# Layer 0 of a four-layer block: routing cut in two parts around its counts, with conv steps, the other half's norms and shared products placed between the parts

## The chip, the core and the metric

The kernel runs on one core of one Trainium2 chip. The metric is device time in microseconds (us). The kernel before takes 1593.74 us as the median of 3 runs (1591.17 to 1594.62).

A core has five engines that each run their own list of instructions in order: PE (TensorE, matmuls, with PEld for its weight loads), DVE (VectorE), ACT (ScalarE), POOL (GpSimd) and SP (SyncE, which here only issues DMAs). They meet at semaphores. An instruction that waits holds up everything behind it on its own engine.

## The reference, cut to what matters

Four layers, each `x = x + attn(norm(x)) + ffn(norm(x))`, on 4096 tokens (16 sequences of 256) of 128 float32 values. Only layer 0 is touched. Its attention is a diagonal state-space recurrence, its feed-forward a mixture of 8 experts with top-2 routing plus one shared expert:

```python
xn = layernorm(x)                                # over 128
# L0 attn: a linear recurrence over time, y = scan(...) @ W_out + b_out
# L0 ffn:
logits = layernorm(xn) @ gate_w.T                # 8 experts
probs = softmax(logits); tk_probs, tk_idx = top_k(probs, 2)
tk_probs = tk_probs / (sum(tk_probs) + 1e-5)
out = swiglu(xn, sWg, sWu, sWd)                  # the shared expert
for e in range(8):
    out = out + w[:, e:e+1] * swiglu(xn, Wg[e], Wu[e], Wd[e])
```

Since the recurrence is linear and the same for all tokens, it is a convolution of each of the 128 channels with a fixed kernel of 256 lags.

## The kernel before, in words

**Tiling.** The tokens lie in 8 blocks `X[0..7]` of 128 x 4 x 128. Layer 0 treats them in two halves (hf 0: blocks 0 to 3, hf 1: blocks 4 to 7), each of 16 row tiles (`HN`).

**What layer 0 does**, by name of its helpers:

- `plain(hf, n, True)` writes a block's normalised rows `xn` by ACT, 4 instructions (L249); `bare(hf, n)` writes the rows that feed the convolution into `Z`, also 4 ACT instructions of L249.
- `turned(hf, n)` transposes a block of `xn` on PE (L149) and copies it to `xT` by ACT (L263). `router(hf, n)` multiplies it with the gate on PE (tile `lg`) and scales it into `logits` on DVE (L280).
- `route(hf)` turns a half's logits into expert slots. Its first part (L311 to L329) is softmax and two arg-maxima, 20 DVE instructions with one exponential on ACT (L314) between them, and ends in `per`, each partition's count per expert. Then PE sums the counts (`tot`, `pos`). The second part (L338 to L382) is DVE again: running positions, tile starts, `slots` (L368), the experts of the slot tiles (`rows_of`, L377), and the two weights of each token (L378 to L382).
- `scatter(hf, n, k)` (L389) sends rows of `xn` to their slots in DRAM (`XS`): 32 indirect DMAs a half, issued by POOL. They need `slots`.
- `toeplitz(g)` (L495) loads a 512 KB tile of lags by SP; 8 buffers, shared with the experts' weights. `conv(q)` does a 16-channel step of the convolution: 64 matmuls into one bank (`cv`), a copy on ACT (L513), a store by SP (L517). It needs all of `Z` and four of the lag tiles. `mix_in(q)` issues the loads for two steps further on and then runs `conv(q)`.
- `share(q)` adds `xn` to block q (L666, DVE) and runs the shared expert: `pg`, `pu` on PE (512 columns, 4 pairs), Silu on ACT (L528), the product on DVE (L529), `py` on PE, and the sum on DVE (L535).
- `lag_levels()` works out what beta and the output bias add: `kf` on ACT (L470), `wb` and `mix` on DVE (L472, L473), PE `lagd`, ACT copy (L478), PE `level`, DVE (L483).

After that come 46 expert tiles of 256 slots each (23 a half): SP loads weights `we` and rows `xs` six tiles ahead, PE does `xsT`, `sg`, `su`, `sy`. Layers 1 to 3 follow.

**What sets the order.** Inside `tc.manual_schedule(engines=ordered)` PE, ACT, DVE and SP keep the order in which the calls are written; POOL is free. Where two such blocks meet, a planner may interleave the end of one with the start of the next on an engine.

**PSUM.** All of layer 0 takes banks from one ring of 8 in the order of allocation, so a new tile waits until the reader of the eighth before it is done.

The written order around the change is: `bare` of all blocks, `route(0)`, scatters of half 0; then a second block: `mix_in(0)`, `plain`/`turned`/`router` of half 1, `mix_in(1)`, `share(0)`, `mix_in(2)`, `share(1)`, `route(1)`, `lag_levels`; scatters of half 1; then a third block with `share(2)` to `share(7)` and `mix_in(3)` to `mix_in(7)` in turn.

Of the kernel before, what the change touches and what calls it, by code (L numbers as in the profile page):

```python
# [51 lines left out]
def program(ctx: ExitStack, tc: tile.TileContext, x, consts, consts0, rows, pk0, w0s, w0e, pk1, pk1i, pk2, pk3, out):  # L52
# [7 lines left out]
    def bank(name):  # L60
        return psum["now"].tile([P, 512], F32, tag="ps", name=name)
# [48 lines left out]
    def mm(o, l, r, start=True, stop=True):  # L110
        nc.tensor.matmul(o, l, r, start=start, stop=stop)  # L111
# [26 lines left out]
    def normalise(dst, src, mv, r, at):  # L138
        for t in range(NT):
            nc.vector.tensor_scalar(  # L140
                dst[:, t, :], src[:, t, :], mv[:, at + t, 0:1], r[:, at + t : at + t + 1],
                ALU.subtract, ALU.mult,
            )
# [45 lines left out]
    with early, banks(8, 0), tc.tile_pool(name="l0", bufs=2) as sp:  # L189
# [15 lines left out]
        for hf in range(2):  # L205
# [3 lines left out]
            n = TILES * SLOTS // P  # L209
# [12 lines left out]
        def clear(hf):  # L222
            for o, i in fills[hf]:
                zeroed[hf].append(nc.sync.dma_start(out=o, in_=i))
# [23 lines left out]
        def rows_by_act(dst, src, r, off, k):  # L248
            nc.scalar.activation(dst, src, AF.Identity, bias=off[:, k : k + 1], scale=r[:, k : k + 1])  # L249

        def plain(hf, n, by_act):
            i = HALVES[hf][n]
            mv, r, _, off, _, _ = mvs[hf]
            if by_act:
                for t in range(NT):
                    rows_by_act(xn[i][:, t, :], X[i][:, t, :], r, off, n * NT + t)
            else:
                normalise(xn[i], X[i], mv, r, n * NT)
# [12 lines left out]
        def router(hf, n):  # L271

            i = HALVES[hf][n]
            if hf not in lgs:
                lgs[hf] = small("logits", hf, HN, E)
            lg = bank(f"lg{i}")
            for t in range(NT):
                mm(lg[:, t * E : (t + 1) * E], xT[i][:, t * P : (t + 1) * P], gates[:, 0])
            ks = slice(n * NT, (n + 1) * NT)
            V.tensor_tensor(  # L280
                lgs[hf][:, ks, :], lg[:, 0 : NT * E].rearrange("p (t e) -> p t e", e=E),
                mvs[hf][5][:, ks].unsqueeze(2).to_broadcast([P, NT, E]), ALU.mult,
            )
# [15 lines left out]
        def route(hf):  # L299


            red = lambda name: sp.tile([P, HN], F32, tag=name, name=f"{name}{hf}", bufs=1)
            full = lambda name: sp.tile([P, HN, E], F32, tag=name, name=f"{name}{hf}", bufs=1)
            per_e = lambda name, *shape: sp.tile([P, *shape], F32, tag=name, name=f"{name}{hf}", bufs=1)
# [22 lines left out]
            V.tensor_tensor(both, oh1, oh2, ALU.add)  # L327
            per = per_e("per", E)
            V.tensor_reduce(per, both.rearrange("p n e -> p e n"), AX.X, ALU.add)  # L329
            tot = bank(f"tot{hf}")  # L330
            mm(tot[:, 0:E], ones2, per)
            pos = bank(f"pos{hf}")
# [88 lines left out]
        def lag_powers():  # L421
            for k in ("fine", "coarse"):
                t = parts[k] = sp.tile([P, 64, 16], F32, tag="h", name=f"lag_{k}", bufs=2)
                V.tensor_tensor(
                    t, parts["rate"].unsqueeze(2).to_broadcast([P, 64, 16]),
                    W0[k].unsqueeze(1).to_broadcast([P, 64, 16]), ALU.mult,
                )
                nc.scalar.activation(t, t, AF.Exp)
# [39 lines left out]
        def lag_levels():  # L468

            nc.scalar.copy(kf, bass.AP(tensor=kb.tensor, offset=kb.offset + 2 * P - 1, ap=[list(kb.ap[0]), [-1, 2 * P]]))  # L470
            wb = sp.tile([P, D], F32, tag="wb", name="wb", bufs=1)
            V.tensor_scalar(wb, W0["wout"], W0["beta"], None, ALU.mult)  # L472
            V.tensor_scalar(mix, W0["wout"], W0["gamma"], None, ALU.mult)  # L473
            ps = bank("lagd")
            for h in range(2):
                mm(ps[:, h * D : (h + 1) * D], kf[:, h * P : (h + 1) * P], wb)
            g = sp.tile([P, 2, D], F32, tag="kb", name="lagd", bufs=1)
            nc.scalar.copy(g, ps[:, 0 : 2 * D].rearrange("p (h d) -> p h d", h=2))  # L478
            ps = bank("level0")
            for h in range(2):  # L480
                for k, (w, at) in enumerate(((W0["upper"], h), (ident, h), (ones2, 0))[0 : 2 + h]):
                    mm(ps[:, h * D : (h + 1) * D], w, g[:, at], k == 0, k == 1 + h)
            V.tensor_tensor(  # L483
                level0, ps[:, 0 : 2 * D].rearrange("p (h d) -> p h d", h=2),
                W0["bout"].unsqueeze(1).to_broadcast([P, 2, D]), ALU.add,
            )
# [4 lines left out]
        def toeplitz(g):  # L491

            toes[g] = sp.tile([P, 4, 256], F32, tag="blk", name=f"toe{g}", bufs=8)
            src = bass.AP(tensor=kd.tensor, offset=kd.offset + g * 4 * 384, ap=[[1, P], [384, 4], [1, 256]])
            return nc.sync.dma_start(out=toes[g], in_=src)  # L495

        def conv(q):

            ps = bank(f"cv{q}")
            for n in range(4):
                toe = toes.pop(4 * q + n)
                for at, k in ((1, 128), (0, 0)):
                    for c in range(4):
                        u = Z[:, at : at + 2, :, 16 * q + 4 * n + c].rearrange("p h b -> p (h b)")
                        mm(
                            ps[32 * c : 32 * c + 32, n * P : (n + 1) * P], u, toe[:, c, k : k + P],
                            n == 0 and at == 1, n == 3 and at == 0,
                        )  # L510
            y = sp.tile([P, 4, P], F32, tag="yc", name=f"yc{q}")
            back = bass.AP(tensor=ps.tensor, offset=ps.offset + P - 1, ap=[list(ps.ap[0]), [P, 4], [-1, P]])
            nc.scalar.copy(y, back)  # L513
            dst = bass.AP(
                tensor=ycd.tensor, offset=ycd.offset + 16 * q * B * S, ap=[[P, P], [4 * B * S, 4], [1, P]]
            )
            nc.sync.dma_start(out=dst, in_=y)  # L517
# [101 lines left out]

        AHEAD = 6  # L620
        NJ = len(jobs)
        ordered = {mybir.EngineType.PE, mybir.EngineType.Activation, mybir.EngineType.DVE, mybir.EngineType.SP}
        with tc.manual_schedule(engines=ordered):
            nc.sync.dma_start(out=kd[:, 256:384], in_=zero[:, 0, :])
            clear(0)
            lag_rates(spread)
            lag_powers()
            spread(0, (1,))
            lag_states()
            lag_sums()  # L630
            spread(0, (2, 3))
            scales(0)
            lag_rows()
            gate_parts()
            plain(0, 0, True)
            plain(0, 3, False)
            plain(0, 1, True)
            turned(0, 0)
            plain(0, 2, True)
            turned(0, 3)  # L640
            turned(0, 1)
            bare(0, 0)
            turned(0, 2)
            spread(1, range(4))
            scales(1)
            for n in (0, 3, 1, 2):
                router(0, n)
            for g in range(8):
                toeplitz(g)
            clear(1)  # L650
            for n in range(1, 4):
                bare(0, n)
            for n in range(4):
                bare(1, n)
            route(0)
        for n in range(HN):
            for k in range(2):
                scatter(0, n, k)

        def mix_in(q):  # L660
            for g in range(4 * q + 8, min(4 * q + 12, 32)):
                toeplitz(g)
            conv(q)

        def share(q):
            V.tensor_tensor(X[q], X[q], xn[q], ALU.add)  # L666
            shared_expert(q)
# [3 lines left out]
            V.tensor_tensor(x4, x4, level0.unsqueeze(1).to_broadcast([P, 2, 2, D]), ALU.add)  # L671

        with tc.manual_schedule(engines=ordered):
            mix_in(0)
            for n in range(4):
                plain(1, n, True)
                turned(1, n)
                if n > 0:
                    router(1, n - 1)
            mix_in(1)  # L680
            router(1, 3)
            share(0)
            mix_in(2)
            share(1)
            route(1)
            lag_levels()
        for n in range(HN):
            for k in range(2):
                scatter(1, n, k)
# [16 lines left out]
        with tc.manual_schedule(engines=ordered | {mybir.EngineType.Pool}):  # L706
# [6 lines left out]
            norms = []  # L713
            for k in range(NJ):
                if k + AHEAD < NJ:
                    fetch_weights(k + AHEAD)
                n = k - TILES - 1
                if 0 <= n < 12:
                    fetch_outputs(0, n)
                if k + AHEAD < NJ:  # L720
                    fetch_slots(k + AHEAD)
                if k + 2 < NJ:
                    turn_slots(k + 2)
                if k + 1 < NJ:
                    up_slots(k + 1)
# [767 lines left out]
```

## Time and profile before

| | |
|---|---|
| median of 3 runs | 1593.74 us |
| the profiled execution | 1487.93 us, of which its span 1486.2 us |
| mean granted TensorE clock of the profiled execution | 0.940 |
| PE busy in the span | 1340.1 us (90%) |
| DVE, ACT, POOL busy | 752.8, 578.4, 214.3 us |
| PE busy, 36.5 to 43.0 us | 0.00 of 6.50 us |
| PE busy, 43.0 to 50.2 us | 1.58 of 7.20 us |
| PE busy, 79.7 to 95.5 us | 7.97 of 15.80 us |
| PE busy, 95.5 to 109.3 us | 5.27 of 13.80 us |
| PE busy, 113 to 157 us | 40.86 of 44.00 us |
| PE busy, 185 to 260 us | 75.00 of 75.00 us |

The profile is of one execution, and all times of single instructions come from it. It ran 106 us faster than the median of the timed runs. Its rows give start, duration, engine, source line, tile and count; "idle before <-X" is how long that engine stood still and which event ended it. Times are counted from the start of the span. In the chain of work that ended last PE holds 79%, DVE 10% and ACT 7%.

### The profile page before, as it was taken

The numbers are of one execution on the slowest core, as the hardware profiler recorded it, in microseconds if no ns is written. First come the engines' busy times: TensorE is split into PE (matmuls) and PEld (weight loads), VectorE is DVE, ScalarE is ACT, GpSimd is POOL, SyncE is SP. The second block draws the span as 40 slices with busy tenths as digits, with TensorE's granted clock in tenths as the row PEclk, the third lists the DMA queues.
The fourth block names the chain that finished last, engine by engine and source line by source line (L and its number), as shares of the span: only waits on it lengthen the run. The fifth ranks groups of instructions, "written<-read, shape, count | busy, mean of one in ns | idle before, by whom it ended". The sixth has DMA issues, their size and how long they took to land.

```text
span 1486.2 us, 28149 instructions
## 1 busy us (share of the span) xinstructions
PE 1340.1 (90%) x11950; PEld 868.6 (58%) x11950; DVE 752.8 (51%) x1636; ACT 578.4 (39%) x898; POOL 214.3 (14%) x218
## 2 busy tenths in 40 slices
PE   3659999969898999899999999999979999999995
PEld 3546899836565666656555445554546666666434
DVE  7355444756666555335732336423375565554364
ACT  5412223334353554321343334333344545543551
POOL 1366004323110000000220112211100000000013
PEclk9979999977798999899999999999978999997998
DMA  7849669640000000000000000000000000000001
GB/s 225 283 135 312 205 178 278 197 152 21 10 11 2 2 2 2 2 1 1 0 1 0 1 0 1 0 0 0 0 1 2 2 2 2 2 2 2 1 1 57
DMA packets 71007, 77.92 MB, mean 52 GB/s; under 512 B 7649, under 2 KB 60258, under 8 KB 70242
## 3 DMA queue, kind: packets, MB, share of 16 engines
q1 hardware_dynamic: 66210, 66.39, 14.5%
q0 software_dynamic: 4240, 8.99, 1.8%
q8 instruction: 94, 1.54, 0.4%
q10 hardware_dynamic: 432, 0.75, 0.2%
q14 instruction: 31, 0.25, 0.1%
HBM read 55.46 MB, written 20.64 MB: 51 GB/s over the span
## 4 chain that ended last, share of the span: by engine, by line
PE 79%; DVE 10%; ACT 7%; issue 2%; DMA 1%; POOL 1%; POOLq 0%; DVEq 0%; SPq 0%; ACTq 0%
PE h L111 15%; PE se L111 9%; PE sc L111 8%; PE po L111 7%; PE av L111 5%; ACT E L920 4%; DVE M L878 3%; PE c L111 3%; PE mT L893 3%; PE sy L111 3%; PE sg L111 2%; PE su L111 2%; PE pq L111 2%; PE pv L111 2%; PE b L111 2%; PE a L111 2%
## 5 line engine op out<-in xcount | busy, mean ns | idle before, releaser
L878 DVE TENSOR_REDUCE M<-sc 128x4 f32<-128x1024 f32 (+3 forms) x256 | 195.9, 818 | 105.0 <-PE sc L111 105.0
L111 PE MATMUL h<-h,pk 128*128 128x512 f32 x512 | 221.0, 592 | 0.0
L920 ACT ACTIVATE E<-se 128x1024 f32<-128x1024 f32 (+1 forms) x192 | 158.8, 879 | 126.0 <-PE se L111 125.7
L111 PEld LDWEIGHTS h<-h,pk 128*128 128x128 f32 x512 | 97.3, 190 | 119.0 <-issue 114.8
L111 PE MATMUL sc<-Kp,Qm 32*128 32x192 f32 (+3 forms) x2048 | 139.8, 358 | 25.0 <-ACT E L920 19.9
L111 PE MATMUL se<-Q,Km 32*128 32x256 f32 (+3 forms) x2048 | 138.4, 355 | 22.4 <-DVE M L878 20.9
L111 PEld LDWEIGHTS sc<-Kp,Qm 32*128 32x128 f32 x2048 | 103.5, 207 | 74.6 <-ACT E L920 33.4
L111 PEld LDWEIGHTS se<-Q,Km 32*128 32x128 f32 x2048 | 99.3, 202 | 62.9 <-issue 51.8
L1098 ACT ACTIVATE h<-h,pk 128x512 f32<-128x512 f32 x64 | 44.0, 687 | 144.3 <-PE h L111 144.2
L1048 POOL TENSOR_TENSOR pr<-q,k 128x512 f32<-128x512 f32 (+2 forms) x24 | 28.3, 1205 | 495.7 <-ACT k L1041 285.8
L601 POOL DMA_INDIRECT yk<-YS,slots x64 | 60.7, 949 | 225.9 <-DMA YS<-ys 95.0
L1108 DVE TENSOR_TENSOR x<-x,po 128x512 f32<-128x512 f32 x8 | 5.5, 688 | 170.5 <-PE po L111 170.5
L111 PE MATMUL av<-E,vals 128*32 128x256 f32 (+3 forms) x2048 | 77.7, 304 | 0.0
L389 POOL DMA_INDIRECT XS<-xn,slots x64 | 63.0, 985 | 73.4 <-DVE slots L368 48.3
L1240 POOL TENSOR_TENSOR xT<-xT,c 128x512 f32<-128x512 f32 x8 | 10.2, 1271 | 389.8 <-DVE c L1239 380.4
L935 ACT COPY cu<-av 128x512 f32<-128x512 f32 x32 | 18.8, 586 | 120.6 <-PE av L111 120.6
L111 PEld LDWEIGHTS av<-E,vals 128*32 128x32 f32 x2048 | 52.9, 111 | 20.0 <-issue 1.6
L583 DVE TENSOR_TENSOR hs<-hs,su 128x512 f32<-128x512 f32 x46 | 31.6, 686 | 57.3 <-PE su L111 57.3
L899 DVE TENSOR_TENSOR Q<-Qp,mT 128x512 f32<-128x512 f32 x32 | 22.0, 688 | 58.0 <-PE mT L893 58.0
L111 PE MATMUL pk<-xT,pk 128*128 128x512 f32 x80 | 47.0, 672 | 3.8 <-ACT Qm L812 3.7
L819 DVE TENSOR_SCALAR Km<-Kp,consts 128x512 f32<-128x512 f32 x64 | 32.2, 545 | 34.6 <-ACT Kp L817 34.6
L111 PEld LDWEIGHTS sy<-we,hs 128*128 128x128 f32 x368 | 47.6, 192 | 2.4 <-DVE hs L583 0.5
(276 smaller groups left out, 2259.0 us busy)
## 6 DMA issues: line engine op xcount, KB each, us to landing
we<-in_w0e SPq DMA_DIRECT2D x46, 384.0 KB, 3.9
toe<-kd SPq DMA_DIRECT2D x32, 512.0 KB, 6.8
xs<-XS SPq DMA_DIRECT2D x46, 128.0 KB, 4.4
YS<-ys SPq DMA_DIRECT2D x46, 128.0 KB, 2.6
XS<-Z SPq DMA_DIRECT2D x4, 1024.0 KB, 9.8
pk<-in_pk SPq DMA_DIRECT2D x1, 3145.5 KB
x<-in_x SPq DMA_DIRECT2D x8, 256.0 KB, 5.2
ycd<-yc SPq DMA_DIRECT2D x8, 256.0 KB, 8.4
```

Source lines behind the costliest of these rows:

```text
L111: nc.tensor.matmul(o, l, r, start=start, stop=stop)
L389: d = nc.gpsimd.indirect_dma_start(out=XS[hf][:, :], out_offset=at_rows(slots[:, hf, k, n : n + 1]), in_=xn[HALVES[hf][n // NT]][:, n % NT ...
L583: nc.vector.tensor_tensor(h, h, pu, ALU.mult)
L601: nc.gpsimd.indirect_dma_start(out=y, out_offset=None, in_=YS[hf][:, :], in_offset=at_rows(slots[:, hf, k, n : n + 1]),)
L819: nc.vector.tensor_scalar(t["Km"][:, T, :, j, :], chunks(t["Kp"][:, T, :]), C["hmask"][:, j : j + 1], C["hone"][:, j : j + 1], ALU.mult, A ...
L878: nc.vector.tensor_reduce(dst, src, AX.X, ALU.max, negate=True)
L893: nc.tensor.transpose(ps[:, T, c * P : (c + 1) * P], negm[bl][:, c, T].rearrange("p g j k -> p (g j k)"), ident)
L899: nc.vector.tensor_tensor(q2, t["Qp"][:, :, o : o + S].rearrange("p t (c q) -> p t c q", c=4), mT[:, :, :, 0, :], ALU.add)
L920: nc.scalar.activation(E[:, 2 * n : 2 * n + 2, :], se[n][:, :, 0 : 2 * wide], AF.Exp, scale=ISQ)
L935: nc.scalar.copy(cu, ps.rearrange("p (t q) -> p t q", t=2))
L1048: nc.gpsimd.tensor_tensor(pr[:, :, j:], q[:, :, j:], k[:, :, 0 : S - j], ALU.mult)
L1098: nc.scalar.activation(hn[:, c, :], ps, AF.Gelu, scale=W2[sn][:, c : c + 1])
```

## The change

`route` and `lag_levels` become generators that stop part-way: `route` after `per` (before PE's count matmuls), `lag_levels` after `wb`/`mix` and again after the copy of `lagd`. In the first block the four `plain(1, n)` and `mix_in(0)` now stand between the two parts of `route(0)`. In the second block the first part of `route(1)` and the start of `lag_levels` move up to stand before `share(0)`; the second part of `route(1)` and the middle of `lag_levels` stand between `mix_in(2)` and `share(1)`; the end of `lag_levels` follows `share(1)`. `mix_in` is defined earlier, unchanged. No instruction that computes something is added or removed. On ACT two table loads fall away, since no exponential stands between Silus any more. SP's and POOL's lists are the same, in the same order.

```diff
             per = per_e("per", E)
             V.tensor_reduce(per, both.rearrange("p n e -> p e n"), AX.X, ALU.add)
+            yield
             tot = bank(f"tot{hf}")
             mm(tot[:, 0:E], ones2, per)
...
             V.tensor_scalar(mix, W0["wout"], W0["gamma"], None, ALU.mult)
+            yield
             ps = bank("lagd")
             for h in range(2):
                 mm(ps[:, h * D : (h + 1) * D], kf[:, h * P : (h + 1) * P], wb)
             g = sp.tile([P, 2, D], F32, tag="kb", name="lagd", bufs=1)
             nc.scalar.copy(g, ps[:, 0 : 2 * D].rearrange("p (h d) -> p h d", h=2))
+            yield
             ps = bank("level0")
...
             for n in range(4):
                 bare(1, n)
-            route(0)
+            routing = route(0)
+            next(routing)
+            for n in range(4):
+                plain(1, n, True)
+            mix_in(0)
+            next(routing, None)
         for n in range(HN):
             for k in range(2):
                 scatter(0, n, k)
...
         with tc.manual_schedule(engines=ordered):
-            mix_in(0)
             for n in range(4):
-                plain(1, n, True)
                 turned(1, n)
                 if n > 0:
                     router(1, n - 1)
             mix_in(1)
             router(1, 3)
+            routing = route(1)
+            next(routing)
+            levels = lag_levels()
+            next(levels)
             share(0)
             mix_in(2)
+            next(routing, None)
+            next(levels)
             share(1)
-            route(1)
-            lag_levels()
+            next(levels, None)
```

Where the first and the second block meet, DVE's list in the built program is not the written one: the four `router(1, n)` rows (L280) and the first rows of the first part of `route(1)` stand inside the second part of `route(0)`. The first L280 stands after `tl` (L355), the second after `st` (L359), the third after `base` (L363), the fourth after `te` (L375). In the built program before, all four stand behind the end of `route(0)`.

More of the change, by code (lines that the diff above doesn't have):

```diff
@@ L621, in program, with mix_in @@
         NJ = len(jobs)
+        def mix_in(q):
+            for g in range(4 * q + 8, min(4 * q + 12, 32)):
+                toeplitz(g)
+            conv(q)
         ordered = {mybir.EngineType.PE, mybir.EngineType.Activation, mybir.EngineType.DVE, mybir.EngineType.SP}
@@ L658, in program @@
                 scatter(0, n, k)
[L660 to L663, printed above, removed]
         def share(q):
```

## The prediction

> **What bounds the kernel now.** First the page's busy times, with the slices of PE and of its granted clock below them.
>
> ```profile
> PE 1340.1 (90%) x11950; PEld 868.6 (58%) x11950; DVE 752.8 (51%) x1636; ACT 578.4 (39%) x898; POOL 214.3 (14%) x218
> ...
> PE   3659999969898999899999999999979999999995
> ...
> PEclk9979999977798999899999999999978999997998
> ```
>
> PE is the bound, except in the first three slices (37.2 us each), where it reads 3, 6, 5. So I read that stretch only: who waits for whom between 36.5 and 113 us.
>
> ```profile
> POOL XS L389 <- DVE slots L368: 48.3, 1, 48.3
> ...
> PE tot L111 <- DVE run L338: 19.4, 2, 12.2
> ACT lagd L478 <- PE lagd L111: 15.9, 1, 15.9
> ...
> PE lagd L111 <- DVE wb L472: 8.0, 1, 8.0
> ```
>
> PE stands still for 27.4 us behind the routing: 12.2 and 7.2 us before the counts of half 0 and half 1 (`tot`; L338 is only the last DVE row before it, `per` is what it needs), and 8.0 us before `lagd`, behind the second part of `route(1)` on DVE. ACT's row is that last wait at second hand; POOL's is the first scatter, which can't start before `slots`. Then PE's own order in time:
>
> ```profile
> 48.62 0.56 PE L111 MATMUL tot<-per,ones 128*128 128x8 f32 x2 [12.17 <-DVE run L338]
> ...
> 50.16 3.76 PE L111 MATMUL cv<-toe,Z 128*32 128x128 f32 x64
> ...
> 66.13 3.72 PE L111 MATMUL cv<-toe,Z 128*32 128x128 f32 x64
> ...
> 79.69 2.26 PE L111 MATMUL cv<-toe,Z 128*32 128x128 f32 x64
> ...
> 95.45 0.59 PE L111 MATMUL tot<-per,ones 128*128 128x8 f32 x2 [7.20 <-DVE run L338]
> ...
> 105.12 1.19 PE L111 MATMUL lagd<-wb,kf 128*128 128x128 f32 x4 [8.02 <-DVE wb L472]
> ...
> 109.26 3.74 PE L111 MATMUL cv<-toe,Z 128*32 128x128 f32 x64
> ...
> 112.93 1.12 PE L111 MATMUL pg<-xT,shared 128*128 128x512 f32 x2
> ```
>
> The last row is `share(2)`. From there PE runs at its own pace (40.9 of 44 us busy to 157, all of 185 to 260), so what counts is how much earlier `share(2)` starts. The conv step takes 3.7 us or 2.26: PE has two speeds. The clock was granted 1.00 from 82 to 92, fell to 0.50 at about 92.4, 4.2 us after `py` ended at 88.25, and came back just before 113. Before 75 us the record says 1.00, but the durations are those of the slow clock, and I go by them.
>
> **The change, part by part.** I write the after-times on the clock of this profile.
>
> *Conv step 0 ahead of the counts.* ACT ends `bare` at 42.93. The lag tiles were issued from 31.0 and landed 4.0 to 9.5 us later, so `cv` starts at 43.0 and ends at 46.8, in time in which PE waited. The counts wait for `per` as now (48.5) and end at 50.2. Removed from the path: 3.76 us.
>
> *The four `plain(1, n)` ahead of the copies.* ACT: 16 rows of 0.39 (1.65 for four) after the exponential, 43.25 to 49.7, then the copy of `cv`, 50.3. Now each `turned` waits for its rows (a period of 2.7 us a block, ACT's 1.65 + 0.59 + a hand-over). After it, from 50.2, only PE counts: 4 transposes of 0.235 (12 took 2.82 at 25.0) make 0.94 a block, a router product 1.71; four and three of them, 3.8 + 5.1 = 8.9, to 59.1. The ACT copies (0.59) lie beside the next block's transposes.
>
> *DVE's new waits.* The interleaved L280 rows make the second part of `route(0)` wait for `lg` at about 53.8, 56.4 and 59.1. Behind the third is the read of `pos` (L364), whose bank `cv` 1 takes, so `cv` 1 starts at 59.7: a loss of 0.6. `slots` comes at about 60.3 instead of 54.9, and the scatters of half 0 (32 x 1.27 = 40.5 us of POOL) end near 101.4 instead of 96.4; those of half 1 follow at once, to about 142 (before: 144). First reader of the former is `xs`, issued at 137.8 now and at about 121 then; `xs` of half 1 comes tens of us later. So this costs nothing while the slack of nearly 20 us holds. `rows_of`, at about 65.5, is read by SP only there too.
>
> `cv` 1 to 63.4, the fourth router product to 65.1, against 71.5 now: 6.4 us gained.
>
> *First part of `route(1)` ahead of `share(0)`.* From L311 to the end of L329 it took 6.5 us (88.89 to 95.40); I add 0.6 for the leftovers of `route(0)` between its rows: 65.2 to 72.3. Then `wb`, `mix` (0.5), L666 (0.68), two L529 (0.69 each): 74.9. This is a loss inside `share(0)`: PE's `pg`/`pu` (8 x 0.96 slow = 7.2, less if it speeds up) end by 71 to 72.4, so `py` waits some 3 us. `py` ends at 74.9 + 1.9 = 76.8, `cv` 2 (2.26) at 79.1. Now that is 81.95. So 2.9 us of the gain stand here, and `per` of half 1 is done.
>
> *Second part of `route(1)` and `lagd` before `share(1)`.* PE: `tot`, `pos` 0.7 at full clock (79.8), `lagd` 0.5, `pg`/`pu` 8 x 0.43 = 3.5, to 83.8. DVE: the second part takes 97.14 to 104.68 = 7.5 us, to 87.4; then L666 and two L529, to 89.5. So PE waits again, about 5 us before `py`, where the whole of `route(1)` and `wb` now cost 7.2 + 8.0. `py` to 91.4, `level` (10 x 0.11) to 92.6, `cv` 3 to 94.9. On DVE the sum L535, slow beside a `cv` (2.2 instead of 0.69), then L483, two L671 and L666 hold `share(2)`'s product by 0.5. `share(2)` thus stands 112.93 - 95.4 = 17.5 us earlier.
>
> *The clock in that 5 us.* The nearest row: the clock fell 4.2 us after PE stopped, so this idle stretch may or may not lower it. [...] At half clock `py` costs 1.5 more, `level` 1.3, `cv` 3 1.5: 4.3 us, a gain of 13.2. By the row at its best 17.5, [...] I take the middle, 15.5. [...]
>
> *Table loads.* Two of 1.28 us go. One ran while ACT waited anyway, the other (113.66) delayed no `py` (first `pg` to last `py` start is 4.55 us with it and without): nothing.
>
> *DMA.* Lag tiles for `cv` 4 are issued at `cv` 2 (77) and needed at 101; from `cv` 3 on the spacing is as now. The DMA engines are 97% busy from 113 to 157 already, but the same bytes come at the same pace.
>
> If PE were slow throughout this stretch, the same addition puts `share(2)` at about 121 before and 102.3 after, 18.7 gained. So the gain is 13 to 19, and 16 the value between. Against the profiled execution that is 1487.9 - 16 = 1472. The timed runs are 106 us longer than it; waits behind DVE and ACT don't stretch with PE's clock, so I take off the same: 1593.7 - 16 = 1578 (1.0%). What a measurement here can tell from no change is about 0.2%, 3 us.
>
> **Rivals.**
>
> 1. *Part of it is given back* (1583 to 1589): the chain through DVE is longer than I add up. For it: in the after-order DVE holds `py` of two `share`s, and each us there is a us of PE; [...] DMA at 97% leaves little room if the scatters now overlap all the conv steps. Against it: the routing's durations are measured twice and agree (6.5 and 7.5 us).
> 2. *No change* (1591 to 1597): the timed runs are 7% slower than the profile. [...] For it: the 106 us. Against it: the slices show 7 to 10 tenths with dips beside idle time, not a level.
> 3. *Slower* (over 1597): the later, dense stages are granted less clock. From 700 to 900 us PE is busy 198.8 of 200 at 1.00; at clock c this costs 200 x (1/c - 1), 16 us at 0.926, so it decides from below about 0.91. No row shows that stage throttled, but the profile is a single execution.
> 4. *The split does nothing*, because DVE's order puts the waits back: then `cv` 1 and `share(0)` start as now, 1590 to 1594. The built order speaks against it: `tot` stands behind `cv` 0, and no L280 stands before `per`.
>
> **How the numbers follow.** My forecast (1574 to 1583) has 0.66; more than that, to 1569, 0.05; rival 1 0.16; rivals 2 and 4 together 0.06; rival 3 0.07. Faster by over 0.2%: 0.66 + 0.05 + 0.16 = 0.87; the same 0.06; slower 0.07. The range 1571 to 1588 takes in the forecast and most of rival 1, and leaves out about 0.17.
>
> **What would show it.** In the profile after: a `cv` of about 3.7 us starts near 43, before `tot`; the wait of `tot` for DVE falls from 19.4 to about 2; `lagd` doesn't wait for `wb`; two waits of `py` for L529, about 3 and 5 us, are new; L280 rows wait inside `route(0)`'s second part, and the first scatter starts near 61; `share(2)`'s `pg` starts at 94 to 100. I am wrong if `pg` of `share(2)` starts after 104, if an `xs` waits for a scatter or a `cv` for its lag tiles, or if `share(2)` starts early and the end doesn't move.

## The result

| | before | after |
|---|---|---|
| median, first measurement | 1592.45 us (4 runs) | 1572.71 us (4 runs) |
| ratio to before | | 0.9883, 95% interval [0.9839, 0.9927] |
| the profiled execution | 1487.93 us | 1570.27 us |
| median, second measurement | 1487.45 us (52 runs) | 1471.37 us (4 runs) |
| ratio to before | | 0.9882, 95% interval [0.9825, 0.9939] |

The change makes the kernel 1.2% faster: 19.7 us in the first measurement, 16.1 in the second. The profile of the kernel after is 82 us longer than the profile of before shown above, although the kernel is faster, because measurements of both kernels come out at one of two levels, some 100 to 110 us apart, and these two profiles were taken at different ones. So the profile after is read first for what makes it long, and then a second profile of the same kernel, taken where before reads 1487, is set against the one of before.

The page of the first profile after, busy times and the slices of PE and of its clock:

```profile
PE 1357.9 (87%) x11950; PEld 874.3 (56%) x11950; DVE 751.0 (48%) x1636; ACT 575.7 (37%) x896; POOL 213.8 (14%) x218
...
PE   3643899886778899999999999999988999999995
...
PEclk9956999997878889979999999999988999997998
```

PE has the same work, and in the third and fourth slice (39.2 us each) it is idle more than before, in the tenth to twelfth somewhat more. The waits of the same stretch as above (36.5 to 113 us; columns: us in total, times, longest) say how:

```profile
PE cv L111 <- issue: 20.7, 18, 1.8
...
PE py L111 <- DVE h L533: 7.5, 1, 7.5
PE cv L111 <- ACT Z L249: 6.6, 1, 6.6
...
PE tot L111 <- DVE run L340: 2.4, 1, 2.4
```

L533 here is the product of `share` that was L529 before (L543 in a kernel of the experiments). The wait of `tot` fell from 19.4 us to 2.4 and that of `lagd` for `wb` is gone, as forecast. New is 20.7 us in which `cv` waits for nothing that the profile shows. In order of time (conv step 2, some of its rows):

```profile
78.61 1.38 PE L111 MATMUL cv<-toe,Z 128*32 128x128 f32 x28
81.03 0.38 PE L111 MATMUL cv<-toe,Z 128*32 128x128 f32 x2 [1.05 <-issue]
81.75 0.27 PE L111 MATMUL cv<-toe,Z 128*32 128x128 f32 x1 [0.34 <-issue]
82.46 0.31 PE L111 MATMUL cv<-toe,Z 128*32 128x128 f32 x1 [0.43 <-issue]
83.89 0.37 PE L111 MATMUL cv<-toe,Z 128*32 128x128 f32 x1 [1.13 <-issue]
...
103.59 0.37 PE L111 MATMUL cv<-toe,Z 128*32 128x128 f32 x1 [1.73 <-issue]
105.69 0.37 PE L111 MATMUL cv<-toe,Z 128*32 128x128 f32 x1 [1.73 <-issue]
106.39 0.37 PE L111 MATMUL cv<-toe,Z 128*32 128x128 f32 x1 [0.33 <-issue]
107.10 1.18 PE L111 MATMUL cv<-toe,Z 128*32 128x128 f32 x16 [0.33 <-issue]
```

28 of the step's 64 matmuls run at the usual pace, then the starts lie 0.7 us or a multiple of it apart until 107.1. The step takes 29.6 us instead of 2.3. Conv step 3 does the same from 125 to 161 us. I call these slow stretches.

### The profile page after: what moved, and what is told of

The parts are those of the page before. It is cut to its first block, busy times and chain, and to the rows that moved or that the text cites. A ratio compares the mean times of both kernels' runs of the same rounds, so it can differ in the third digit from the quotient of the medians.

```text
span 1568.5 us, 28145 instructions
## 1 busy us (share of the span) xinstructions
PE 1357.9 (87%) x11950; PEld 874.3 (56%) x11950; DVE 751.0 (48%) x1636; ACT 575.7 (37%) x896; POOL 213.8 (14%) x218
## 4 chain that ended last, share of the span: by engine, by line
PE 75%; DVE 9%; ACT 6%; issue 5%; DMA 2%; another core or an unknown queue 1%; POOL 1%; SPq 0%; POOLq 0%; DVEq 0%; ACTq 0%
PE h L111 14%; PE se L111 9%; PE sc L111 7%; PE po L111 7%; PE av L111 5%; ACT E L933 4%; DVE M L891 3%; PE c L111 3%; PE mT L906 3%; PE sg L111 2%; PE sy L111 2%; PE su L111 2%; PE pq L111 2%; PE cv L111 2%; PE pv L111 2%
## 5 line engine op out<-in xcount | busy, mean ns | idle before, releaser
L605 POOL DMA_INDIRECT yk<-YS,slots x64 | 60.7, 948 | 293.0 <-DMA xs<-XS 133.4
L111 PE MATMUL cv<-toe,Z 128*32 128x128 f32 x512 | 36.1, 335 | 53.9 <-issue 47.2
L111 PEld LDWEIGHTS cv<-toe,Z 128*32 128x32 f32 x512 | 23.6, 195 | 64.9 <-issue 57.5
L111 PE MATMUL sg<-xsT,we 128*128 128x256 f32 x184 | 48.4, 386 | 6.1 <-issue 6.1
L111 PE MATMUL sy<-we,hs 128*128 128x128 f32 x368 | 49.0, 276 | 2.9 <-DVE hs L587 2.5
```

The lines of the kernel that those rows point to most:

```text
L605: nc.gpsimd.indirect_dma_start(out=y, out_offset=None, in_=YS[hf][:, :], in_offset=at_rows(slots[:, hf, k, n : n + 1]),)
```

## The experiments

**Both kernels again, and each half of the change alone.** The first question is whether the slow stretches come from the change; the second, whether its two halves add up as the prediction has them. The two partial kernels are cut from the kernel after. Half 0 alone keeps the first block as it is and puts the rest back:

```diff
             router(1, 3)
-            routing = route(1)
-            next(routing)
-            levels = lag_levels()
-            next(levels)
             share(0)
             mix_in(2)
-            next(routing, None)
-            next(levels)
             share(1)
-            next(levels, None)
+            for _ in route(1):
+                pass
+            for _ in lag_levels():
+                pass
```

Half 1 alone puts the first block back and keeps the second:

```diff
-            routing = route(0)
-            next(routing)
-            for n in range(4):
-                plain(1, n, True)
-            mix_in(0)
-            next(routing, None)
+            for _ in route(0):
+                pass
...
+            mix_in(0)
             for n in range(4):
+                plain(1, n, True)
                 turned(1, n)
```

Expected of before, of after, of half 0 and of half 1:

> The kernel before, unchanged. Theory A (stretches in which PE gets one instruction per 0.7 us, seen in the profile after at 80 to 107 and 125 to 161 us, are a state that falls on both kernels): a second profile of the kernel before shows such stretches too, 60 to 110 us in sum, and its profiled execution reads 1580 to 1597 us instead of 1488. Theory B (the change makes these stretches): its profile shows none and reads 1484 to 1492. Timed ratio 1.000 by both.

> The kernel after, unchanged. Theory A: ratio 0.985 to 0.993; the profile shows slow PE stretches, 60 to 110 us in sum, not of need at the same places; what is left without them is 1470 to 1480. Theory B: the stretches lie again in conv steps 2 and 3, 28 and 37 us long within 3 us.

> Only half 0's routing is cut in two (plain rows and conv step 0 between its parts); half 1's routing and the levels stand as before. By the prediction's steps: the fourth router product ends 6.4 us earlier, so 6 us faster than before (ratio 0.996), and no py waits for the first part of route(1). By rival 1 (the gain is given back inside share(0)): ratio 1.000.

> Only half 1's routing and the levels are cut and moved; half 0 stands as before. By the prediction's steps: 17.5 - 6.4 = 11 us at full clock, 7 at half clock, so 9 us faster (ratio 0.994); py waits for L533 twice, about 3 and 5 us. By rival 1: the two waits eat it, ratio 0.998 to 1.000.

| kernel | median | ratio to before (1487.45 us) | `share(2)` starts |
|---|---|---|---|
| before | 1487.66 us | 1.000 [0.9981, 1.0019] | 109.1 us |
| half 0 alone | 1479.58 us | 0.9941 [0.9925, 0.9958] | 99.1 us |
| half 1 alone | 1480.04 us | 0.9939 [0.9920, 0.9958] | 103.6 us |
| after | 1471.37 us | 0.9882 [0.9825, 0.9939] | 95.7 us |

The profile of before shown ahead of the prediction has `share(2)` at 112.9, this one at 109.1: PE was at its faster pace earlier in it (the first `pg` of `share(0)` took 1.10 us instead of 2.05, `cv` 3 2.74 instead of 3.74). So the same row can differ by some 4 us from one profile of a kernel to the next.

None of the four profiles has a slow stretch, and all times lie at the lower level. So neither theory was right as put: the stretches are not the change's doing (B), but they were not in this profile of before either (A). The halves gain 7.9 and 7.4 us (forecast: 6 and 9), 15.3 in sum, against 16.1 for both together. The waits of the kernel after in this measurement, 36.5 to 113 us:

```profile
PE py L111 <- DVE h L533: 11.2, 4, 5.1
...
PE cv L111 <- ACT Z L249: 8.6, 1, 8.6
PE tot L111 <- DVE run L340: 2.0, 1, 2.0
```

and PE's rows in it:

```profile
43.09 3.77 PE L111 MATMUL cv<-toe,Z 128*32 128x128 f32 x64 [8.55 <-ACT Z L249]
48.83 0.56 PE L111 MATMUL tot<-per,ones 128*128 128x8 f32 x2 [1.97 <-DVE run L340]
...
58.69 3.68 PE L111 MATMUL cv<-toe,Z 128*32 128x128 f32 x64
62.30 1.06 PE L111 MATMUL lg<-gates,xT 128*128 128x8 f32 x8
63.22 1.10 PE L111 MATMUL pg<-xT,shared 128*128 128x512 f32 x2
...
72.02 3.95 PE L111 MATMUL py<-shared,h 128*128 128x128 f32 x16 [5.12 <-DVE h L533]
75.90 2.31 PE L111 MATMUL cv<-toe,Z 128*32 128x128 f32 x64
...
78.91 0.61 PE L111 MATMUL lagd<-wb,kf 128*128 128x128 f32 x4
...
87.83 3.95 PE L111 MATMUL py<-shared,h 128*128 128x128 f32 x16 [4.87 <-DVE h L533]
...
93.43 2.30 PE L111 MATMUL cv<-toe,Z 128*32 128x128 f32 x64
95.66 1.12 PE L111 MATMUL pg<-xT,shared 128*128 128x512 f32 x2
```

The conv step stands in the wait for the counts, `lagd` follows `pos` without a wait, and both waits of `py` for L533 are there. In the order and the kind of its waits this is the account of the prediction; their sizes are compared further down.

**What is left: PE waiting for DVE twice.** From the kernel after, half 1's routing is cut into six pieces behind its exponential, and each `share` from 0 to 5 takes one of them behind its two L533 rows, where DVE waits for `py` anyway. With it the scatters of half 1 move behind `share(5)` and SP's first six fetches ahead of the `yT` loads. (The `yield`s of the pieces and the old place of the scatters are left out of the diff.) The other kernel moves one call only: `share(0)` ahead of the first part.

```diff
-        def shared_expert(i):
+        def shared_expert(i, step):
...
+            next(step, None)
             xf = X[i].rearrange("p t d -> p (t d)")
             nc.vector.tensor_tensor(xf, xf, py, ALU.add)
...
         def share(q):
             V.tensor_tensor(X[q], X[q], xn[q], ALU.add)
-            shared_expert(q)
+            shared_expert(q, steps["routing"])
...
+            steps["routing"] = routing
             share(0)
             mix_in(2)
-            next(routing, None)
             next(levels)
             share(1)
             next(levels, None)
...
                     share(q)
                     level_in(q)
+                if q == 5:
...
+                    for n in range(HN):
+                        for k in range(2):
+                            scatter(1, n, k)
...
+            for k in range(AHEAD):
+                fetch_weights(k)
+                fetch_slots(k)
             yT = wp.tile([P, 2, B, P], F32, tag="Z", name="yT")
```

```diff
+            share(0)
             routing = route(1)
             next(routing)
             levels = lag_levels()
             next(levels)
-            share(0)
             mix_in(2)
```

Expected of the six pieces, of `share(0)` first, and of the kernel after beside them:

> From the kernel after: what is left of the routing of half 1 on DVE is cut in six pieces of 1.5 to 2.9 us, one put behind the two L533 rows of each of share(0) to share(5), where DVE waits for py anyway; the scatters of half 1 follow share(5), and SP's first six fetches stand ahead of the yT loads. Theory A (what is left in this stretch is PE waiting twice for DVE, 5.1 and 4.9 us in the last profile of the kernel after, with py at half clock behind each, 2 x 1.9 us): both waits go, share(2) starts near 82 instead of 95.7, and the time is 1457 to 1462 us where the kernel after takes 1471 (ratio to before 0.979 to 0.983). Theory C (the gain of the change came from elsewhere, or time taken out here is given back by the clock later): 1468 to 1474.

> From the kernel after: share(0) stands ahead of the first part of route(1) instead of behind it. Theory A (the 6.5 us of the first part are on PE's path wherever they stand in one piece): py of share(0) no longer waits 5 us for L533, but tot waits some 6 to 7 us for per, and share(2) starts 0 to 2 us later than in the kernel after; ratio to before 0.988 to 0.990. Theory C (the place before share(0) is what costs): 4 to 6 us faster than the kernel after, 0.984 to 0.986.

> The kernel after, unchanged, as the mark for the two others. Ratio to before 0.986 to 0.991. If PE's slow stretches (one instruction per 0.7 us, 28 and 37 us long in the first profile of the kernel after, none in the second) come back, before and after both read some 65 to 110 us more.

This measurement fell on the upper level: before 1596.56 us, six pieces 1571.43, `share(0)` first 1571.40, after 1570.33 (ratios 0.9849, 0.9845, 0.9853, their intervals overlap). So at this level the three are alike, and all have the two slow stretches. What was expected of the lower level could not be read here, so the first two ran once more later:

> The six-piece kernel again, unchanged. Where the kernel before reads 1487: theory A (PE's two waits for DVE were what was left) 1457 to 1462, ratio 0.980 to 0.983, share(2) starts near 82; theory C 1468 to 1474, ratio 0.987 to 0.991. Where it reads 1590: 1569 to 1574.

> share(0) ahead of the first part of route(1), again, unchanged. Where the kernel before reads 1487: theory A 1471 to 1474 (tot waits 6 to 7 us in place of py's 5, share(2) starts near 96); theory C 1465 to 1468. Where it reads 1590: 1569 to 1576.

There before read 1487.53. The six pieces took 1460.77 us, ratio 0.9788 [0.9738, 0.9838], as theory A has it (1457 to 1462): 26.8 us faster than before and some 10.6 faster than the kernel after in the second measurement. `share(0)` first took 1473.12, 0.9894 [0.9842, 0.9945], also as A has it. The two intervals touch, but all four runs of the six pieces (1452 to 1463) lie below all four of `share(0)` first (1468 to 1479). PE's rows of the six pieces and then of `share(0)` first:

```profile
63.59 2.42 PE L111 MATMUL py<-shared,h 128*128 128x128 f32 x16 [1.03 <-DVE h L543]
...
73.16 1.83 PE L111 MATMUL py<-shared,h 128*128 128x128 f32 x14 [0.63 <-DVE h L543]
...
78.25 1.12 PE L111 MATMUL pg<-xT,shared 128*128 128x512 f32 x2
...
84.47 0.29 PE L111 MATMUL tot<-per,ones 128*128 128x8 f32 x2
```

```profile
66.30 1.83 PE L111 MATMUL py<-shared,h 128*128 128x128 f32 x14 [0.19 <-DVE h L533]
...
76.90 0.57 PE L111 MATMUL tot<-per,ones 128*128 128x8 f32 x2 [6.54 <-DVE per L330]
...
87.46 3.87 PE L111 MATMUL py<-shared,h 128*128 128x128 f32 x16 [3.84 <-DVE h L533]
```

In pieces the routing costs PE no wait over 1.03 us, `py` of `share(0)` takes 2.42 us where it took 3.95, and `share(2)` starts at 78.3. The scatters of half 1 start at 102.0, against 102.9 in the kernel after, so at this level their new place is not what gained. Of the 17.4 us that `share(2)` gains over the kernel after, 14.2 are left at the first expert tile (125.5 against 139.7) and 10.6 in the time; where the rest goes was not followed. With the first part in one piece behind `share(0)`, the first `py` doesn't wait, but `tot` waits 6.5 us in its place: the stall moves, it doesn't go.

**The slow stretches.** In four profiles at the upper level (after twice, six pieces, `share(0)` first) each slow stretch ended 5 to 6 us after the last scatter of a half was issued (101.8 and 107.1; 154.9 and 160.7 us in the first). So the scatters are the suspect. One kernel leaves them out: nothing is written into the experts' slots, which stay zero, and the slot reads wait for the zero fills alone.

```diff
         def scatter(hf, n, k):
-            d = nc.gpsimd.indirect_dma_start(
-                out=XS[hf][:, :], out_offset=at_rows(slots[:, hf, k, n : n + 1]),
-                in_=xn[HALVES[hf][n // NT]][:, n % NT, :], in_offset=None,
-            )
...
+            pass
...
-            for s in scatters[hf]:
-                tc.add_manual_dep(d.ins, s.ins.name, sync, reason="slots filled")
+            for z in zeroed[hf]:
+                tc.add_manual_dep(d.ins, z.ins.name, sync, reason="zeros")
```

Beside it ran before, for its profile, and the six pieces:

> From the kernel after: both halves' scatters (64 indirect DMAs of POOL) are left out, so the experts work on zero rows; all else stands. Theory S (PE's slow stretches come from the scatters under way: in each of four profiles they end 5 to 6 us after the last scatter of a half is issued): no slow stretch is left, whatever the condition of the chip: 1465 to 1475, also where the kernel before reads 1590. Theory I (PE's instructions come late for a reason of their own): where the kernel before reads 1590, this reads 1565 to 1575 with two slow stretches in it. Where the kernel before reads 1487, both say 1465 to 1475.

> The kernel before, unchanged, for its profile. Where it reads 1590: by theory S its conv step 2 is slow until 5 to 6 us after the last scatter of half 0 (about 102), the second part of route(1) then follows share(1) and route(1)'s first part, slots of half 1 come near 125, and a second slow stretch ends near 170, some 10 us later than in the kernel after in the same condition (158 to 161). Where it reads 1487: no slow stretch. Ratio 1.000 in both.

> The kernel of the run before with the same pieces (half 1's routing in six pieces), unchanged. Where the kernel before reads 1487: 1457 to 1462 by theory A, 1468 to 1474 by theory C, as stated for it. Where it reads 1590: 1569 to 1574 again, because by theory S the end is then set by the scatters of half 1, which start at 140 there.

It was the upper level again (before 1594.44). Before itself took 1593.99 (1.0007 [0.9984, 1.0029]), the six pieces 1572.53 (0.9858 [0.9809, 0.9906]), and the kernel without scatters 1505.08 (0.944 [0.939, 0.949]). It has no slow stretch: `share(2)` starts at 93.1 us and the first expert tile at 137.1, where the lower level has 95.7 and 139.7 for the kernel after with its scatters:

```profile
73.43 2.28 PE L111 MATMUL cv<-toe,Z 128*32 128x128 f32 x64
...
90.92 2.27 PE L111 MATMUL cv<-toe,Z 128*32 128x128 f32 x64
93.12 1.13 PE L111 MATMUL pg<-xT,shared 128*128 128x512 f32 x2
```

So at this level both slow stretches were gone when the scatters were left out. The number expected, 1465 to 1475, was missed: some 34 us are left against the lower level. They lie where POOL's 64 gathers run (indirect DMAs that fetch the experts' results; L605 in the kernel after, L596 here). From the first gather to the last, 220.6 us pass instead of 187.7 in the kernel after at the lower level. The stretch from the first expert tile to the first gather takes 82.4 against 81.3, the one from the last gather to the first `h` of layer 1 301.5 against 297.8. While the gathers run, DVE and ACT wait for signals whose sender the profile does not name ("remote"); the kernel after at the lower level has no such wait of these engines there:

```profile
DVE M L882 <- remote: 10.2, 3, 5.0
...
ACT xsT L567 <- remote: 8.1, 2, 7.7
ACT cu L939 <- remote: 7.9, 1, 7.9
```

That the gathers cause this was not shown: they were not taken out.

The profile of before at this level, where scatters of half 0 end:

```profile
99.39 0.37 PE L111 MATMUL cv<-toe,Z 128*32 128x128 f32 x1 [1.03 <-issue]
100.09 0.37 PE L111 MATMUL cv<-toe,Z 128*32 128x128 f32 x1 [0.33 <-issue]
100.79 0.37 PE L111 MATMUL cv<-toe,Z 128*32 128x128 f32 x1 [0.33 <-issue]
101.49 1.09 PE L111 MATMUL cv<-toe,Z 128*32 128x128 f32 x11 [0.33 <-issue]
```

Here it is conv step 1 that is held, from 68.3 to 101.5 us, 6 us past the last scatter at 95.5. Everything behind it follows late: `share(0)` at 104, `tot` at 128.3, the first scatter of half 1 at 135.5, and the second slow stretch ends at 181.7. In the kernel after (its two profiles at this level) conv step 2 is held instead, the counts of half 1 follow it at once, its scatters start at 112.7 and 115.4, and the second stretch ends at 158 and 161. The first expert tile comes at 219.6 before and at 204.2 and 206.9 after. The expectation had the second stretch of before end near 170; it ended later because the first stretch caught conv step 1, ahead of `share(0)`, and not step 2.

## Why the prediction was right

Forecast 1578 (1571 to 1588), measured 1572.71 from a before of 1592.45. As a difference: 16 forecast, 19.7 measured at the upper level and 16.1 at the lower. At the level of the profile it was worked out from, the forecast for a kernel's time, 1472, met 1471.4. By its steps, in that profile:

- *Conv step 0 ahead of the counts*: right; it ran from 43.1 to 46.9.
- *DVE's new waits*: the three L280 rows came at 53.9, 56.4 and 58.8 (53.8, 56.4, 59.1 forecast) and the first scatter at 61.3. That this costs nothing was right at the lower level. The 0.6 us that `cv` 1 was to lose to the bank of `pos` was wrong: it starts at 58.69, ahead of the read of `pos` (L366 here) at 59.0.
- *Fourth router product*: forecast to end at 65.1, ended at 63.2: `cv` 1 had started 1.0 us earlier than forecast, and this product took 1.06 us, where the third took 1.71.
- *First part of `route(1)`*: 65.2 to 72.3 forecast, 63.6 to 70.4 found, its length nearly right. The wait of `py` was 5.1 us instead of 3: `pg` and `pu` ran at a granted clock of 1.00 (63 to 67 us), so PE was done with them at 66.9 and not at 71 or later, and only waited longer for the same DVE chain.
- *Second part*: the wait of 5 us was 4.9.
- *The clock*: this is the term that was mis-sized. It fell from 1.00 to 0.50 in both gaps, also in the first, which the prediction put at 3 us and gave no such cost: there it fell 2.1 us after PE had stopped. Both `py` took 3.95 us, 2 more than at a clock of 1.00, where the forecast had 1.5. The half clock lasted 6.8 us each time; but PE stood still for 3.0 and 1.7 us of that, so `level` lost only 0.7 us and `cv` 3 (2.30) nothing. The cost was 2.0 + 2.5 us, where the forecast had 0 to 4.3, at the second gap alone.
- *Sum*: `share(2)` at 95.66, where the forecast had 95.4 with no cost of the clock and 99.7 with all of it. As the clock cost 4.5 us, the other steps were forecast some 4 us too late: the fourth router product by 1.9, and `py`, which starts behind the first of a pair of L533 rows (72.02, the pair runs from 71.28 to 72.56) and not behind both. That these errors nearly cancel is luck. The row is 17.3 us earlier than in the profile worked from, 13.4 earlier than in the second one of before; the timed gain, 16.1, lies between.
- *Rival 1* was right in kind (DVE holds two `py`, and the six pieces win that back), but the two waits were already in the forecast and no further loss came. *Rival 2*'s sign, the 106 us between profile and timed runs, was misread: of the 100 us between the two levels of the kernel after, some 66 go when the scatters are left out (1571 to 1505), and some 33 more lie in the stretch of the gathers, which were not taken out. *Rival 3* did not come: a dense stretch of 464 us (618 to 1082 in the profile of before, 700 to 1165 in the first after) had a granted clock of 1.00 in both. *Rival 4* did not come either: `cv` 0 stands in the wait for the counts.

One step was right only in its result. "I take off the same" from the longer timed runs held, 19.7 us, but not for the reason given. Rows of DVE and ACT did keep their length: in the profile of before L319 to L322 take 0.29 us each at a clock of 1.00 (starting at 91.1 to 92.1) and 0.28 to 0.29 at 0.50 (93.1 to 94.1), and the ACT copy of `cv` took 0.59 us at 1.00 (82.07) as at 0.50 (161.36 in the first profile after). But at the upper level conv steps stand in the slow stretches (29.6 us for step 2 instead of 2.3). What the profiles show instead is that half 1's scatters start some 20 us earlier and the second slow stretch ends 21 to 24 us earlier. The six pieces, 10 us better at the lower level, bear this out: in their first profile at the upper level `share(2)` starts at 116.3, 42 us ahead of the kernel after in the same measurement (158.5), but half 1's scatters start at 140.0 instead of 112.7, the second slow stretch ends at 185.6 instead of 158, and the first expert tile comes only 4 us earlier (200.4 against 204.2). That the scatters' start is the whole of the gain there was not tested by moving them alone.

## What to carry to other kernels

Here a chain of short DVE instructions ahead of PE's next work cost most of its length in each place where it stood in one piece (for half 1's routing waits of 7.2 and 8.0 us before, 5.1 and 4.9 after, 6.5 and 3.8 with `share(0)` first). Cut at the points where DVE waited anyway, it cost PE at most 1.0 us at a time (1488 us before, 1471 with the change, 1461 with six pieces). When a profile's own time and the timed runs differ by several per cent, work out the gain in the profile, but look for the row that makes the difference before trusting it elsewhere: here an improvement of 10 us at one level was worth nothing at the other. Look also for what else is under way when an engine waits for "issue".

## What the runs showed of the hardware that was not expected

**PE and DVE stood still in some measurements while POOL's scatters ran.** At the upper level PE's instructions start only 0.7 us or a multiple of it apart while the scatters are under way, for 27 to 37 us at a time; in the first profile after, DMA moved 57 GB/s in the one stretch (79.5 to 108 us) and 60 in the other (124 to 161). PE is not alone. DVE's sum L539 needs nothing later than `py`, and came 13.7 us after `py` had ended in the kernel after beside the six pieces (88.5 against 74.8 us):

```profile
DVE x L539 <- remote: 17.1, 1, 17.1
```

In the first profile of the six pieces the same sum (L550 there) waited twice in this way, 12.0 us at the longest. POOL issues its scatters 1.27 us apart in the first profile after (94.19, 95.45, 96.72 us) as in the one of before at the lower level (57.37, 58.64, 59.91). In other measurements the same program with the same scatters shows no trace of it. All kernels of one measurement were at the same level, and a measurement is one chip; the chip with the same number was at the lower level once and at the upper once. Why only some measurements have these stretches, and how the waits come about, was not shown.

**The clock fell 2.1 to 4.1 us after PE stopped.** Granted clock of the kernel after at the lower level (columns: stretch, length, busy time of PE, PEld, DVE, ACT, POOL, clock, DMA share, GB/s):

```profile
63.00:67.00 4.00, 3.90 (x12) 1.63 (x11) 3.29 (x17) 2.36 (x5) 3.09 (x4) 1.00 0.99 275
67.00:69.00 2.00, 0.00 (x0) 0.00 (x0) 1.78 (x7) 0.65 (x2) 1.58 (x2) 1.00 1.08 378
69.00:71.00 2.00, 0.00 (x0) 0.00 (x0) 1.87 (x7) 0.00 (x0) 1.50 (x2) 0.51 0.81 266
```

PE ended `pu` at 66.9 and the clock fell at 69.0, 2.1 us later; at the second gap it took 3.1, in the profile of before 4.1. PE went on at 72.02 and 87.83, and the clock was back at 1.00 at 75.9 and 92.9, 3.8 and 5.1 us later.

The lengths of `py` behind its waits at the lower level: after 5.1 and 4.9 us in the kernel after, 3.95 us both times; after 3.3 us with half 1 alone, 3.17; after 3.8 us with `share(0)` first, 3.87; after 1.03 us in the six pieces, 2.42. Where it waited 0.6 us for L533 in the kernel after (100.21 and 108.75), the 14 rows behind the wait took 1.83 us.

PE's pace also fell without a wait: in the kernel with half 0 alone PE's rows from 50.55 to 59.84 us show none, and yet `cv` 1 took 3.77 us (56.15), where `cv` 2 took 2.30 (67.05), right behind a router product of 0.96 us and transposes of 0.63 us for four, which take 1.71 and 1.09 in the kernel after. What set the time of these changes was not shown.
